# Strassen's seven products for the q, k, v, g projections of layer 0

## The chip, the cores and the metric

The kernel runs on one core of a Trainium2 chip. The metric is the device time of one execution in microseconds, and the comparison is by the median of several runs. All data are float32.

## The reference

The input `x` is 1 x 128 x 256 x 256: 128 rows (`s`) of 256 tokens with 256 channels. Two layers follow each other, each a group norm and an attention over the 256 tokens of each row, added to `x`. Cut to what matters:

```python
# layer 0: 8 heads of 32 channels, with a bias from pair_repr and a gate
gate = sigmoid(xn @ gate_proj)
q, k, v = split(xn @ qkv_proj, 3)            # 256 x 256 each
sim = softmax(q @ k.T / sqrt(32)) + bias     # bias: pair_repr @ bias_proj
x = x + ((sim @ v) * gate) @ out_proj
# layer 1: 4 heads of 64 channels, scores kept only in a band |i - j| <= 16
x = x + softmax(banded(q @ k.T / 8)) @ v @ w_out.T + b_out   # q, k, v with biases
```

The group norm (32 groups of 8 channels) needs statistics over all of `x` before layer 0 starts, and over all of layer 0's output before layer 1 starts.

## The kernel before

There are three stages. The first streams `x` and `pair_repr` through SBUF by DMA: VectorE (DVE) takes the statistics of `x`, TensorE (PE) turns `pair_repr` and forms the bias of the 8 heads, which stays in SBUF (`bias_sb`). The second is layer 0, row by row; its output goes to DRAM (`x1`). The third is layer 1, two rows at a time.

In layer 0 a row lies as channels by tokens: two halves of 128 channels on the partitions, 256 tokens along the free axis. For each row `s`:

- `piece(s, 0)` fetches the row in groups of `XG` = 4 rows (`load`, on SP's queue), turns it on DVE (`turned`, L474) and normalises it on DVE (`normalized`, L464) into `xn`.
- `piece(s, 1..4)` are the projections q, k, v, g. Each is a 256 x 256 by 256 product, made of four matmuls of 128 x 128 weights with 256 columns (`by_channel`, L484; for v `by_token`, L495). ScalarE (ACT) copies each result from PSUM (L542, L547); for g it takes exp(-g) on the way (L552).
- `scores(s, half)` makes the scores of four heads (`sim`, L561), their exponentials on ACT (`ex`, L568) and, on DVE, the sum over the two halves of the keys (`both`, L571).
- `attend(s)` makes the softmax's sums (`zs`, L585), the bias times v (`bv`) and the exponentials times v (`av`, L597). ACT copies `zs` to `z` (L603). DVE forms `d` = (1 + exp(-g)) z (L605), its reciprocal (L609), `t` (L607, L608) and `at` (L611), and a minimum for a check (`zmin`, L613).
- `finish(s)` projects `at` by `out_sb` (`po`, L484), adds the row on DVE (L623), takes the statistics for layer 1 every second row (L626) and stores four rows at a time (L628).

The order of the work is written out in the loop at L635: for each `s` it is scores(s, 0), attend(s - 1), scores(s, 1), the projections of s + 1, finish(s - 1), piece(s + 2, 0). A scheduler may move instructions within this order where the data allow. The PSUM banks are a ring of five that `sim`, the projections and `po` share (`proj_bank`, `sim_bank`), beside one each for `zs`, `bv` and `av`. A bank is taken again when its last reader is done.

GpSimd (POOL) loads the weights and builds masks at the start, and in layer 1 it multiplies the exponentials by the band mask (L717) and adds their halves (L724). It cannot reach PSUM. Weights that need turning are loaded to `w_raw` by `load_weights`, in the first stage.

Of the kernel before, what the change touches and what calls it, by code (L numbers as in the profile page):

```python
# [15 lines left out]
P = 128  # L16
R = 256
# [22 lines left out]
def conv_preact_kernel(  # L40
# [105 lines left out]
    bias_sb = const.tile([P, 2, H0, R], F32, name="bias_sb")  # L146
    zmin = const.tile([P, 2 * S], F32, name="zmin")
# [142 lines left out]
    XG = min(4, S)  # L290
# [7 lines left out]
    GROUPS = [1, 1, 2] + [XG] * (S // XG - 1)  # L298
# [11 lines left out]
    with ExitStack() as early:  # L310
# [6 lines left out]
        w_raw = prt_pool.tile([P, 8, C], F32, name="w_raw", bufs=1)  # L317
# [4 lines left out]
        def load_weights():  # L322
            nc.gpsimd.dma_start(out=w_raw[:, 6:8, :], in_=out_w.rearrange("(t p) c -> p t c", p=P))
# [108 lines left out]
        for m in range(NM):  # L432
# [17 lines left out]
            if m == NM // 4:  # L450
                load_weights()
            if m == NM * 3 // 4:
                turn_weights()
# [48 lines left out]
    SG = min(4, S)  # L502
# [8 lines left out]
    with ExitStack() as both:  # L511
# [5 lines left out]
        def load1(g):  # L517
            if g * XG < S and g not in ygs:
                yg = big1.tile([P, XG, 2, R], F32, tag="yg", name=f"yg{g}", bufs=3)
                nc.sync.dma_start(out=yg, in_=rows(x1, g * XG, XG))  # L520
                ygs[g] = yg

        with ExitStack() as lay0:
# [4 lines left out]
            def piece(s, n):  # L528
                if s >= S:
                    return  # L530
                if n == 0:
                    g, k = ROWS[s]
                    if k == 0:
                        load(g + 1)
                    xt = row.tile([P, 2, R], F32, tag="xt", name=f"xt{s}", bufs=5)
                    turned(xt, xgs[g], k)
                    st[s] = {"xt": xt, "xn": normalized(row, xt, mean0, rstd0, f"0_{s}")}
                elif n in (1, 2):
                    w = "qk"[n - 1]
                    ps = by_channel(qkv_sb, (n - 1) * C, st[s]["xn"], f"p{w}{s}")  # L540
                    a = row.tile([P, 2, R], F32, tag=w, name=f"{w}{s}")
                    nc.scalar.copy(a, ps)  # L542
                    st[s][w] = a
                elif n == 3:
                    ps = by_token(st[s]["xn"], qkv_sb, 2 * C, f"pv{s}")
                    v = row.tile([P, 2, C], F32, tag="v", name=f"v{s}", bufs=3)
                    nc.scalar.copy(v, ps)  # L547
                    st[s]["v"] = v
                elif n == 4:
                    ps = by_channel(gate_sb, 0, st[s]["xn"], f"pg{s}")  # L550
                    e = row.tile([P, 2, R], F32, tag="e", name=f"e{s}", bufs=3)
                    nc.scalar.activation(e, ps, AF.Exp, scale=-1.0)  # L552
                    st[s]["e"] = e

            def scores(s, half):
                q, k = st[s]["q"], st[s]["k"]
                sims = [sim_bank(f"sim{s}_{half}_{j}") for j in range(4)]
                for kt in range(2):
                    for j in range(4):
# [3 lines left out]
                            lhsT=k[p0 : p0 + D0, half, kt * P : (kt + 1) * P], rhs=q[p0 : p0 + D0, half, :],  # L563
# [3 lines left out]
                for j in range(4):  # L567
                    nc.scalar.activation(ex[:, j], sims[j], AF.Exp, scale=1.0 / math.sqrt(D0))  # L568
                both = att.tile([P, 4, R], F32, tag="both", name=f"both{s}_{half}", bufs=3)
                for j in range(0, 4, 2):  # L570
                    nc.vector.tensor_tensor(both[:, j : j + 2], ex[:, j : j + 2, 0, :], ex[:, j : j + 2, 1, :], ALU.add)  # L571
                hd[s, half] = (ex, both)

            def attend(s):
                if s < 0:
                    return
                (ex0, both0), (ex1, both1) = hd.pop((s, 0)), hd.pop((s, 1))
                v = st[s]["v"]

                zs = ps_av.tile([P, 2, R], F32, tag="z", name=f"zs{s}")  # L580
                bv0 = ps_av.tile([P, 2, R], F32, tag="bv", name=f"bv{s}")
                av = ps_av.tile([P, 2, R], F32, tag="av", name=f"av{s}")
                for half, both in enumerate((both0, both1)):
# [5 lines left out]
                for to, weights in (  # L589
# [432 lines left out]
```

## Time and profile before

| | us |
|---|---|
| median of 6 runs | 3367.05 (3364.84 to 3368.4) |
| profiled execution | 3364.23 |
| its span, first to last instruction | 3362.5 |
| PE busy | 3278.7 (98%) |
| DVE busy | 2461.1 (73%) |
| ACT busy | 1479.9 (44%) |
| POOL busy | 416.5 (12%) |

The span is one execution on the core. Matmuls are pipelined and their ends are modelled, so a busy PE is not PE at its peak. A group's line in the profile gives source line, engine, operation, output and inputs, shapes and count, then busy us, mean ns of one, and the idle time before it with what ended it. A float32 matmul shows as two instructions.

### The profile page before, as it was taken

The numbers are of one execution on the slowest core, as the hardware profiler recorded it, in microseconds if no ns is written. First come the engines' busy times: TensorE is split into PE (matmuls) and PEld (weight loads), VectorE is DVE, ScalarE is ACT, GpSimd is POOL, SyncE is SP. The second block draws the span as 40 slices with busy tenths as digits, with TensorE's granted clock in tenths as the row PEclk, the third lists the DMA queues.
The fourth block names the chain that finished last, engine by engine and source line by source line (L and its number), as shares of the span: only waits on it lengthen the run. The fifth ranks groups of instructions, "written<-read, shape, count | busy, mean of one in ns | idle before, by whom it ended". The sixth has DMA issues, their size and how long they took to land.

```text
span 3362.5 us, 83261 instructions
## 1 busy us (share of the span) xinstructions
PE 3278.7 (98%) x36809; PEld 2585.2 (77%) x36809; DVE 2461.1 (73%) x3794; ACT 1479.9 (44%) x3162; POOL 416.5 (12%) x347
## 2 busy tenths in 40 slices
PE   6799999999999999999999999899999999999997
PEld 4477777777777777777777777688888888888886
DVE  4757777777777777777777777657777777777777
ACT  4554444444444444444444444344444444444442
POOL 2000000000000000000000000033333333333332
PEclk9999999999999999999999999999999999999999
DMA  9932212112121121121121110012222122222221
GB/s 382 411 74 51 64 26 51 27 28 49 26 39 39 26 39 39 26 47 30 26 51 27 36 42 14 14 39 54 56 71 58 52 71 58 53 70 58 60 63 40
DMA packets 343296, 209.12 MB, mean 62 GB/s; under 512 B 270600, under 2 KB 336144, under 8 KB 336656
## 3 DMA queue, kind: packets, MB, share of 16 engines
q1 hardware_dynamic: 342032, 201.36, 22.4%
q8 instruction: 290, 4.75, 0.6%
q0 software_dynamic: 752, 2.36, 0.2%
q14 instruction: 78, 0.64, 0.1%
q10 hardware_dynamic: 144, 0.00, 0.0%
HBM read 136.59 MB, written 67.11 MB: 61 GB/s over the span
## 4 chain that ended last, share of the span: by engine, by line
PE 93%; DMA 3%; DVE 3%; issue 0%; ACT 0%; SPq 0%; DVEq 0%; ACTq 0%
PE sim L561 8%; PE pq L484 7%; PE p1v L686 7%; PE 1po L484 7%; PE p1q L484 7%; PE p1k L484 7%; PE po L484 7%; PE pg L484 7%; PE pv L495 7%; PE pk L484 7%; PE bv L597 6%; PE av L597 6%; PE zs L585 4%; DMA xs<-in_x_dram 3%; PE 1sim L707 3%; PE 1avz L739 2%
## 5 line engine op out<-in xcount | busy, mean ns | idle before, releaser
L568 ACT ACTIVATE ex<-sim 128x512 f32<-128x512 f32 x1024 | 528.7, 603 | 643.9 <-PE sim L561 643.6
L764 DVE RECIPROCAL 1rz<-1z 128x512 f32<-128x512 f32 x128 | 427.8, 3342 | 174.1 <-ACT 1z L762 174.1
L609 DVE RECIPROCAL d<-d 128x512 f32<-128x512 f32 x128 | 427.9, 3343 | 0.0
L571 DVE TENSOR_TENSOR both<-ex 128x512 f32<-128x512 f32 x512 | 333.9, 682 | 74.0 <-ACT ex L568 74.0
L717 POOL TENSOR_TENSOR 1p<-1ex,seen 128x768 f32<-128x768 f32 x128 | 233.8, 1827 | 740.4 <-ACT 1ex L715 740.4
L561 PE MATMUL sim<-q,k 32*128 32x256 f32 x4096 | 294.9, 401 | 0.2 <-ACT ex L568 0.2
L464 DVE TENSOR_SCALAR xn<-xt,mean,rstd 128x256 f32<-128x256 f32 x256 | 94.1, 409 | 265.1 <-PE pg L484 265.0
L561 PEld LDWEIGHTS sim<-q,k 32*128 32x128 f32 x4096 | 186.1, 184 | 101.2 <-DVE zmin L613 51.0
L678 ACT ACTIVATE 1q<-p1q,bqk 128x256 f32<-128x256 f32 x256 | 107.2, 470 | 345.3 <-PE p1q L484 345.3
L484 PE MATMUL pq<-xn,qkv_sb 128*128 128x256 f32 x1024 | 255.5, 393 | 0.0
L484 PE MATMUL po<-at,out_sb 128*128 128x256 f32 x1024 | 245.7, 384 | 10.1 <-DVE at L611 10.1
L663 POOL MEMSET 1p<- 128x1216 f32 x4 | 4.3, 1111 | 1997.3 <-DVE at L611 1997.3
L484 PE MATMUL 1po<-1at,w_out_t 128*128 128x256 f32 x1024 | 241.6, 390 | 5.3 <-DVE 1at L766 5.3
L484 PE MATMUL p1q<-xn,w_in_t 128*128 128x256 f32 x1024 | 244.1, 382 | 2.0 <-DVE xn L464 1.1
L597 PE MATMUL bv<-bias_sb,v 128*32 128x256 f32 x4096 | 244.4, 379 | 0.0
L597 PE MATMUL av<-ex,v 128*32 128x256 f32 x4096 | 244.4, 379 | 0.0
L484 PE MATMUL p1k<-xn,w_in_t 128*128 128x256 f32 x1024 | 243.0, 381 | 0.0
L484 PE MATMUL pg<-xn,gate_sb 128*128 128x256 f32 x1024 | 241.9, 379 | 0.0
L495 PE MATMUL pv<-qkv_sb,xn 128*128 128x256 f32 x1024 | 241.9, 379 | 0.0
L484 PE MATMUL pk<-xn,qkv_sb 128*128 128x256 f32 x1024 | 241.9, 379 | 0.0
L686 PEld LDWEIGHTS p1v<-w_in_t,xn 128*64 128x64 f32 x4096 | 222.3, 137 | 21.5 <-issue 21.5
L686 PE MATMUL p1v<-w_in_t,xn 128*64 128x128 f32 x4096 | 238.0, 274 | 0.0
(157 smaller groups left out, 5192.4 us busy)
## 6 DMA issues: line engine op xcount, KB each, us to landing
pr<-in_L_conv_pair_repr_dram SPq DMA_DIRECT2D x32, 1024.0 KB, 23.4
x<-o SPq DMA_DIRECT2D x32, 1024.0 KB, 4.4
yg<-x SPq DMA_DIRECT2D x32, 1024.0 KB, 5.8
out_dram<-1o SPq DMA_DIRECT2D x256, 128.0 KB, 3.6
xg<-in_x_dram SPq DMA_DIRECT2D x124, 256.0 KB, 5.8
xs<-in_x_dram SPq DMA_DIRECT2D x15, 2048.0 KB, 21.4
xs<-in_x_dram SPq DMA_DIRECT2D x2, 1024.0 KB, 17.7
qkv_sb<-in_L_conv_qkv_proj_dram POOLq DMA_DIRECT2D x4, 192.0 KB, 13.1
```

The lines of the kernel that those rows point to most:

```text
L484: nc.tensor.matmul(ps[:, m, :], lhsT=w[:, kt, col + m * P : col + (m + 1) * P], rhs=xn[:, kt, :], start=(kt == 0), stop=(kt == 1),)
L495: nc.tensor.matmul(ps[:, t, :], lhsT=a[:, kt, t * P : (t + 1) * P], rhs=w[:, kt, col : col + C], start=(kt == 0), stop=(kt == 1),)
L561: nc.tensor.matmul(sims[j][:, kt, :], lhsT=k[p0 : p0 + D0, half, kt * P : (kt + 1) * P], rhs=q[p0 : p0 + D0, half, :], start=True, stop=True,)
L568: nc.scalar.activation(ex[:, j], sims[j], AF.Exp, scale=1.0 / math.sqrt(D0))
L571: nc.vector.tensor_tensor(both[:, j : j + 2], ex[:, j : j + 2, 0, :], ex[:, j : j + 2, 1, :], ALU.add)
L585: nc.tensor.matmul(zs[D0 * j : D0 * (j + 1), half, :], lhsT=ones[:, 0:D0], rhs=both[:, j, :], start=True, stop=True,)
L597: nc.tensor.matmul(to[D0 * j : D0 * (j + 1), half, :], lhsT=v[:, kt, h * D0 : (h + 1) * D0], rhs=weights(h, kt), start=(kt == 0), stop=(kt ...
L609: nc.vector.reciprocal(d, d)
L678: nc.scalar.activation(a[:, half, :], ps[:, half, :], AF.Identity, bias=b)
L686: nc.tensor.matmul(ps[KB * half : KB * (half + 1), b, :], lhsT=xn[:, kt, KB * b : KB * (b + 1)], rhs=w_in_t[:, kt, 2 * C + P * half : 2 * ...
L717: nc.gpsimd.tensor_tensor(p.rearrange("p j (r c) -> p (j r) c", c=WROW)[:, :, 0 : 2 * WSTEP] .rearrange("p r (t c) -> p r t c", c=WSTEP)[: ...
L764: nc.vector.reciprocal(rz, z)
```

## The change

Two rows are projected at once. Call the rows A and B, each with its two halves of channels x0 and x1, so that the product with one projection's weights (w00, w10, w01, w11, each 128 x 128) is a 2 x 2 block product. Strassen's scheme with shared sums makes it with seven block products where the plain form has eight. The sums of weights are made once, in the first stage, by GpSimd (`sum_weights`). The four sums of a pair's rows (`sum_rows`, into `ts`) and the last sums of the results (`Seven.add`) are made by GpSimd for each pair.

`stretch` is the new order of two projections, q and k after even rows, v and g after odd ones, for the pair of rows ahead. Each of the two has one PSUM bank in which sums grow over products 1, 5, 6, 3, 7, 4. ACT copies it out (`take`) after 5, after 6, after 7 and after 4, and the products 2 of both go to a third bank, copied as `two`. The exponentials of the second half of the scores (`weigh`) are placed between these steps. exp(-g) is taken in place for a pair of rows at once. A v product has its row sum as the weights, and so is two matmuls with 128 columns.

`attend` is split: `sum_heads` (`zs` and `bv`) stands before scores(s, 1), `av` and the DVE steps after it. The groups of rows are two, not four (`XG`), in `load`, in the stores and in layer 1's loads, where the buffers are five, not three. `w_raw` is taken from the ring of the `pair_repr` tiles. Layer 1's output tile shares the ring of layer 0's.

The diff, cut to its core:

```diff
+    NS = ("s1", "s2", "s3", "s4", "n11")
+    sums = {w: const.tile([P, len(NS), P], F32, name=f"sums_{w}") for w in "qkvg"}
+    def quarter(w, kt, m):
+        source, col = (gate_sb, 0) if w == "g" else (qkv_sb, "qkv".index(w) * C)
+        return source[:, kt, col + m * P : col + (m + 1) * P]
+    def sum_weights():
+        for w in "qkvg":
+            s1, s2, s3, s4, n11 = (sums[w][:, n, :] for n in range(len(NS)))
+            w00, w10, w01, w11 = (quarter(w, kt, m) for m in range(2) for kt in range(2))
+            nc.gpsimd.tensor_tensor(s1, w01, w11, ALU.add)
+            nc.gpsimd.tensor_tensor(s2, s1, w00, ALU.subtract)
+            nc.gpsimd.tensor_tensor(s3, w00, w01, ALU.subtract)
+            nc.gpsimd.tensor_tensor(s4, w10, s2, ALU.subtract)
+            nc.gpsimd.tensor_scalar(n11, w11, -1.0, None, op0=ALU.mult)
+    def stationary(w, n):
+        if n <= 2:
+            return quarter(w, n - 1, 0)
+        return sums[w][:, NS.index({3: "s4", 4: "n11", 5: "s1", 6: "s2", 7: "s3"}[n]), :]
...
-    XG = min(4, S)
+    XG = 2
...
-    GROUPS = [1, 1, 2] + [XG] * (S // XG - 1)
+    GROUPS = [1, 1] + [XG] * (S // XG - 1)
...
-        w_raw = prt_pool.tile([P, 8, C], F32, name="w_raw", bufs=1)
...
         def load_weights():
+            w_raw = pr_pool.tile([P, 8, C], F32, tag="pr", name="w_raw")
...
                 load_weights()
+                sum_weights()
...
-                yg = big1.tile([P, XG, 2, R], F32, tag="yg", name=f"yg{g}", bufs=3)
+                yg = big1.tile([P, XG, 2, R], F32, tag="yg", name=f"yg{g}", bufs=5)
...
+            xns, tss, res = {}, {}, {}
+            def normal(s):
                 if s >= S:
                     return
...
+                g, k = ROWS[s]
+                if k == 0:
+                    load(g + 1)
+                xt = row.tile([P, 2, R], F32, tag="xt", name=f"xt{s}", bufs=6)
+                turned(xt, xgs[g], k)
+                st[s] = {"xt": xt}
+                i, r = divmod(s, 2)
+                if r == 0:
+                    xns[i] = row.tile([P, 4, R], F32, tag="xn", name=f"xn{i}")
+                for half in range(2):
+                    nc.vector.tensor_scalar(
+                        xns[i][:, 2 * r + half, :], xt[:, half, :],
+                        mean0[:, half : half + 1], rstd0[:, half : half + 1],
+                        op0=ALU.subtract, op1=ALU.mult,
+                    )
+            def sum_rows(i):
+                if 2 * i >= S:
+                    return
+                x, t = xns[i], row.tile([P, 4, R], F32, tag="ts", name=f"ts{i}", bufs=1)
+                nc.gpsimd.tensor_tensor(t[:, 0], x[:, 2], x[:, 0], ALU.subtract)
+                nc.gpsimd.tensor_tensor(t[:, 1], x[:, 3], t[:, 0], ALU.subtract)
+                nc.gpsimd.tensor_tensor(t[:, 2], x[:, 3], x[:, 2], ALU.subtract)
+                nc.gpsimd.tensor_tensor(t[:, 3], t[:, 1], x[:, 1], ALU.subtract)
+                tss[i] = t
+            class Seven:
+                def __init__(self, w, i):
+                    self.w, self.i = w, i
+                    self.to = row.tile([P, 4, R], F32, tag=w, name=f"{w}{i}")
+                    res[w, i] = self.to
+                    self.mid = row.tile([P, 2, R], F32, tag="mid", name=f"mid{w}{i}")
+                def open(self):
+                    self.ps = proj_bank(f"p{self.w}{self.i}")
+                def product(self, n, two=None):
+                    x, t = xns[self.i], tss[self.i]
+                    moving = {1: x[:, 0], 2: x[:, 1], 3: x[:, 3], 4: t[:, 3], 5: t[:, 0], 6: t[:, 1], 7: t[:, 2]}[n]
+                    out = two if n == 2 else self.ps[:, 1 if n in (3, 5) else 0, :]
+                    first = n == 1 or (n == 2 and self.w in "qv")
+                    flags = dict(stop=n in (2, 3, 4), skip_group_check=True)
+                    if self.w != "v":
+                        nc.tensor.matmul(out, lhsT=stationary(self.w, n), rhs=moving, start=first, **flags)
+                        return
+                    for t2 in range(2):
+                        cols = slice(t2 * P, (t2 + 1) * P)
+                        nc.tensor.matmul(
+                            out[:, cols], lhsT=moving[:, cols], rhs=stationary(self.w, n),
+                            start=first and t2 == 0, **flags
+                        )
+                def take(self, what):
+                    if what == "15":
+                        nc.scalar.copy(self.to[:, 0:4:3, :], self.ps)
+                    elif what == "6":
+                        nc.scalar.copy(self.mid[:, 0, :], self.ps[:, 0, :])
+                    elif what == "7":
+                        nc.scalar.copy(self.mid[:, 1, :], self.ps[:, 0, :])
+                    else:
+                        nc.scalar.copy(self.to[:, 1:3, :], self.ps)
+                def add(self, two):
+                    nc.gpsimd.tensor_tensor(self.to[:, 0], self.to[:, 0], two, ALU.add)
+                    nc.gpsimd.tensor_tensor(self.to[:, 2:4], self.to[:, 2:4], self.mid, ALU.add)
...
+                def weigh(j):
                     nc.scalar.activation(ex[:, j], sims[j], AF.Exp, scale=1.0 / math.sqrt(D0))
-                both = att.tile([P, 4, R], F32, tag="both", name=f"both{s}_{half}", bufs=3)
-                for j in range(0, 4, 2):
-                    nc.vector.tensor_tensor(both[:, j : j + 2], ex[:, j : j + 2, 0, :], ex[:, j : j + 2, 1, :], ALU.add)
+                    if j % 2 == 1:
+                        nc.vector.tensor_tensor(
+                            both[:, j - 1 : j + 1], ex[:, j - 1 : j + 1, 0, :], ex[:, j - 1 : j + 1, 1, :], ALU.add
+                        )
+                return weigh
...
+            def products(to, s, weights):
+                i, r = divmod(s, 2)
+                v = res["v", i]
+                for half in range(2):
+                    for kt in range(2):
+                        for j in range(4):
+                            c0 = kt * P + j * D0
+                            nc.tensor.matmul(
+                                to[D0 * j : D0 * (j + 1), half, :],
+                                lhsT=v[:, 2 * r + half, c0 : c0 + D0], rhs=weights(4 * half + j, kt),
+                                start=(kt == 0), stop=(kt == 1),
+                            )
+            def sum_heads(s):
                 if s < 0:
                     return
                 zs = ps_av.tile([P, 2, R], F32, tag="z", name=f"zs{s}")
                 bv0 = ps_av.tile([P, 2, R], F32, tag="bv", name=f"bv{s}")
+                for half in range(2):
+                    both = hd[s, half][1]
                     for j in range(4):
                         nc.tensor.matmul(
                             zs[D0 * j : D0 * (j + 1), half, :], lhsT=ones[:, 0:D0], rhs=both[:, j, :],
                             start=True, stop=True,
                         )
+                products(bv0, s, lambda h, kt: bias_sb[:, kt, h, :])
+                hd[s] = (zs, bv0)
...
+            def stretch(names, i, weigh=None, s=-1):
+                weigh = weigh or (lambda j: None)
+                if 2 * i >= S:
+                    for j in range(4):
+                        weigh(j)
+                    if s >= 0:
+                        finish(s, by_channel(out_sb, 0, st[s]["at"], f"po{s}"))
+                    return
+                f, g = (Seven(w, i) for w in names)
+                f.open()
+                f.product(1)
+                f.product(5)
+                weigh(0)
+                g.open()
+                g.product(1)
+                g.product(5)
+                weigh(1)
+                f.take("15")
+                twos = proj_bank(f"p2{names}{i}")
+                f.product(2, twos[:, 0, :])
+                g.product(2, twos[:, 1, :])
+                g.take("15")
+                weigh(2)
+                f.product(6)
+                g.product(6)
+                f.take("6")
+                weigh(3)
+                f.product(3)
+                g.product(3)
+                g.take("6")
+                two = row.tile([P, 2, R], F32, tag="two", name=f"two{names}{i}")
+                nc.scalar.copy(two, twos)
+                f.product(7)
+                g.product(7)
+                f.take("7")
+                g.take("7")
+                f.product(4)
+                g.product(4)
+                f.take("34")
+                g.take("34")
+                po = by_channel(out_sb, 0, st[s]["at"], f"po{s}") if s >= 0 else None
+                for n, p in enumerate((f, g)):
+                    p.add(two[:, n, :])
+                if s >= 0:
+                    finish(s, po)
+            for s in range(2):
+                normal(s)
+            sum_rows(0)
+            stretch("qk", 0)
+            for s in range(2, 4):
+                normal(s)
             for s in range(S + 1):
                 if s < S:
-                    scores(s, 0)
+                    weigh = scores(s, 0)
+                    if s == 0:
+                        stretch("vg", 0, weigh)
+                        sum_rows(1)
+                    else:
+                        for j in range(4):
+                            weigh(j)
+                sum_heads(s - 1)
+                weigh = scores(s, 1) if s < S else None
                 attend(s - 1)
-                if s < S:
-                    scores(s, 1)
-                for n in range(1, 5):
-                    piece(s + 1, n)
-                finish(s - 1)
+                if s % 2 == 0 and s < S:
+                    e = res["g", s // 2]
+                    tc.keep_in_program_order(nc.scalar.activation(e, e, AF.Exp, scale=-1.0))
+                stretch(("qk", "vg")[s % 2], s // 2 + 1, weigh, s - 1)
                 if s == S - 2:
                     most1 = join_most(st1, stats1, 1)
                     load1(0)
                     load1(1)
-                piece(s + 2, 0)
+                if s % 2 == 1:
+                    normal(s + 3)
+                    normal(s + 4)
+                    sum_rows((s + 3) // 2)
...
-                    o = big1.tile([P, 2, 2, R], F32, tag="o1", name=f"1o{s}")
+                    o = big1.tile([P, 2, 2, R], F32, tag="o", name=f"1o{s}")
```

In the built program PE's order in a row is: sim (half 0), zs, bv, sim (half 1), av, products 1 and 5 of the first matrix, 1 and 5 of the second, both 2, both 6, 3 of the second, 3 of the first, both 7, the first matmul of `po`, both 4, the rest of `po`. DVE's order is: `o`, in every second row the statistics, the transposes and `xn` of a row ahead, both `both` of half 0, `d`, `zmin`, the reciprocal, the two `t`, the first `both` of half 1, `at`, the second `both`.

## The prediction

> **What bounds the kernel now.** First the engines' busy time and the chain that ended last: TensorE is busy nearly all the span, and the chain runs through it.
>
> ```profile
> PE 3278.7 (98%) x36809; PEld 2585.2 (77%) x36809; DVE 2461.1 (73%) x3794; ACT 1479.9 (44%) x3162; POOL 416.5 (12%) x347
> PE 93%; DMA 3%; DVE 3%; issue 0%; ACT 0%; SPq 0%; DVEq 0%; ACTq 0%
> ```
>
> Then the windows by stage (length, then busy us and instructions of each engine, granted clock, DMA share and GB/s). The stage of layer 0's rows, which the change rewrites, has PE busy in 1955.8 of 1956 us at full clock. DVE is the runner-up, and GpSimd does nothing in it.
>
> ```profile
> 202.00:2158.00 1956.00, 1955.76 (x19220) 1455.43 (x19219) 1472.41 (x2022) 882.43 (x1777) 0.00 (x0) 1.00 0.17 36
> ```
>
> Last the timeline of one row of that stage (start, length, engine, line, operation): from one first `sim` to the next.
>
> ```profile
> 1200.65 1.15 PE L561 MATMUL sim<-q,k 32*128 32x256 f32 x16
> 1201.73 1.07 PE L585 MATMUL zs<-both,ones 128*32 128x256 f32 x16
> 1202.61 1.91 PE L597 MATMUL bv<-bias_sb,v 128*32 128x256 f32 x32
> 1204.34 1.91 PE L597 MATMUL av<-ex,v 128*32 128x256 f32 x32
> 1206.18 1.15 PE L561 MATMUL sim<-q,k 32*128 32x256 f32 x16
> 1207.26 2.00 PE L484 MATMUL pq<-xn,qkv_sb 128*128 128x256 f32 x8
> 1209.09 1.89 PE L484 MATMUL pk<-xn,qkv_sb 128*128 128x256 f32 x8
> 1210.81 1.89 PE L495 MATMUL pv<-qkv_sb,xn 128*128 128x256 f32 x8
> 1212.54 1.89 PE L484 MATMUL pg<-xn,gate_sb 128*128 128x256 f32 x8
> 1214.27 1.89 PE L484 MATMUL po<-at,out_sb 128*128 128x256 f32 x8
> 1216.09 1.15 PE L561 MATMUL sim<-q,k 32*128 32x256 f32 x16
> ```
>
> And the lines of DVE's timeline in the same row that count below:
>
> ```profile
> 1201.48 1.29 DVE L626 BATCH_NORM_STATS2 stats<-o 128x6 f32<-128x512 f32 x2
> ...
> 1205.73 3.34 DVE L609 RECIPROCAL d<-d 128x512 f32<-128x512 f32 x1
> ...
> 1210.45 0.69 DVE L611 TENSOR_TENSOR at<-t,d 128x512 f32<-128x512 f32 x1
> ...
> 1214.47 0.73 DVE L464 TENSOR_SCALAR xn<-xt,mean,rstd 128x256 f32<-128x256 f32 x2 [2.12 <-PE pg L484]
> ```
>
> A row takes 15.44 us, and PE goes from group to group without a hole. `at`, which `po` needs, is done at 10.5 us into the row (1211.14), and `po` starts at 13.6. So DVE has 3.1 us in hand. That margin is what the change spends.
>
> **The sum goes against the profiled execution**: 3364.2 us, its span 3362.5 and 1.7 around it. That is 2.8 below the median of 3367.05, added back at the end. A measurement of this kernel can tell about 0.2% from no change, 6.7 us.
>
> **Removed.** The four projections are 32 instructions per row, 0.216 us apart (pk to pv: 1.72 for 8). Seven products for eight leave 28: 0.863 us off a row, 110.5 over 128 rows. A row bound by PE is then 14.58. The built program has these 28, so the change does what it says.
>
> **v in halves.** Each v product is two matmuls of 128 columns, so a full weight load comes every half step: 28 loads in a pair of rows where 14 wider steps would do. Two rows bound this, p1v of layer 1 on the page (busy us, mean ns) and pz in the timeline of the first stage:
>
> ```profile
> L686 PE MATMUL p1v<-w_in_t,xn 128*64 128x128 f32 x4096 | 238.0, 274 | 0.0
> ```
>
> ```profile
> 171.66 3.66 PE L389 MATMUL pz<-ident,pr 128*128 128x128 f32 x32
> ```
>
> pz has full 128x128 loads at 128 columns: (3.66 - 0.3)/31 = 0.108 a step, just half of 0.216, so no loss. p1v (two halves side by side) is 238/2048 = 0.116, or 0.22 us a pair, 14 in all. I take pz: 0. The 14 stays in the range.
>
> **ScalarE and the accumulators.** One bank is evacuated four times in the middle of its sums (after products 5, 6, 7 and 4), so PE and ScalarE take turns on it. ScalarE's copies per row go from four of 0.6 to five of 0.6 and four of 0.47, and every second row gets an exponential of 128x1024 (about 1.1): some 10 us in a row with the rest, not a bound. The turn counts. In the built order q's product 3 waits until its product 6 is copied out: ScalarE starts 0.2 after the next group has begun on PE (pk at 1209.09, the copy of q at 1209.29), its copy takes 0.47 (L678's mean) and may first have to wait for the copy of both products 2, and only k's 6 and 3 (0.86) lie between. Likewise 4 after 7, where the first step of `po` was placed as filler. I count 0.1 a row, bounds 0 and 0.4 (each turn short by 0.2): 12.6 us, 126 rows.
>
> **DVE's margin.** Counted from the row's first `sim`, three things move `at`. `xn` now stands ahead of the two `both` of half 0, 0.65 later. One `both` of half 1 stands ahead of `at`, 0.6 later. `av` moves behind the second `sim`, which DVE, still in its reciprocal, does not feel. So in rows with the statistics (1.2 us, every second) `at` ends at 10.5 + 1.25 = 11.75, in the others near 11.0. And `po` is wanted sooner: av ends near 6.6, then twelve products of 0.432, so its first step falls at 11.8, and products 4 of both matrices are queued behind it. The 3.1 us are gone: 0 to 0.1 left.
>
> **GpSimd.** Per pair of rows it gets four row sums and, for each matrix, an add of 256 and one of 512 elements. Its nearest rows:
>
> ```profile
> L717 POOL TENSOR_TENSOR 1p<-1ex,seen 128x768 f32<-128x768 f32 x128 | 233.8, 1827 | 740.4 <-ACT 1ex L715 740.4
> L724 POOL TENSOR_TENSOR 1zp<-1p 128x512 f32<-128x512 f32 x128 | 162.6, 1270 | 10.0
> ```
>
> The step is 2.18 ns an element beside 0.15 fixed, so 0.71 us for 256. 8 x 0.71 + 4 x 1.27 = 10.8 us in 29: the work fits, and q, k, v, g have a row's slack. The row sums come ready by about 5 us of a row, products 5 wait for them at 7.0. So nothing is lost by GpSimd's own time.
>
> What it may cost is on DVE. The first two adds of a stretch start when the copy of both products 2 is out, at 10.1 us, and run to 11.5. That is just when DVE does `both` and `at`, each reading two SBUF tensors, as GpSimd does. No row shows the two together: GpSimd was idle in layer 0, and layer 1's DVE steps read at most one tensor of SBUF. Those are no slower for it (xn 411 ns in layer 1, 409 in layer 0), so the lower end is 0. The upper end is that each step shuts the other out for its whole length, in turns. Odd rows: `both` (due 10.4) waits to 10.8, `at` waits for the second add, 12.0 to 12.7, and `po` is 0.9 late: 15.49 a row. Even rows come to the same, since GpSimd's late adds and row sums already push `both` of half 0. In between, only the part that grows with size excludes (0.56 of 0.71 for GpSimd, 0.53 of 0.60 for DVE): `both` to 10.65, second add from 11.2, `at` from 11.75 to 12.4, `po` 0.54 late: 15.12 a row. I take this one. The layer 1 rows argue for 0 but are of another kind, and two engines on the same memory for the same half microsecond argue for a price. Below nothing it cannot be: a wait shortens no step.
>
> The Trainium skill speaks against the change here. Its page "SBUF — State Buffer", section "Who interferes with whom", says that a VectorE instruction with two SBUF inputs and a GpSimd instruction that reads SBUF shut each other out, the first keeping the shared pair for the whole instruction. No row of this trace shows it or denies it. By that rule the sum would be the upper end, 3380, by layer 1's rows 3278.
>
> **Ends.** Start: two rows must be normalised and a GpSimd sum made before product 5, and row 0 carries two stretches: 3 us. End: row 126 has no projections left to cover it. PE has 8.5 us of work there, while `at` and `po` need about 13.5: 5 us. The weights' staging tile takes one of the five `pr` buffers while DMA is the bound (396 GB/s): 0 to 2.6 us (1 MB at that rate), 1 taken. Twenty weight sums run on an idle GpSimd early: 0. Groups of two rows, not four, double the issues on SP and halve each load. A group is still fetched one pair (29 us) ahead and xg landed in 5.8 us: 0. Together 9.
>
> **Sum:** 3364.2 - 110.5 + 126 x 0.54 + 9 = 3330.7, and 2.8 for the median: **3334**. (The 0.1 of ScalarE's turns falls within the later wait for `at`.)
>
> **Rivals.**
> *No contention.* The 0.54 is then 0.1: 3364.2 - 110.5 + 12.6 + 9 + 2.8 = 3278. For it: layer 1's unchanged DVE steps. Against: they read one tensor.
> *Full exclusion (slower).* One mechanism, at the wait of `po` for `at`: 0.91 a row, 3380. Where DVE also loses each tie it is 1.26 (15.84 a row), 3424. It decides against the change from 0.81 us a row on, (110.5 - 9)/126. For it: DVE's margin is gone and all falls at the one spot. Against: it needs whole instructions, start-up included, to exclude.
>
> **How the numbers follow.** Partial exclusion 0.38, no contention 0.26, full exclusion 0.28, something unpriced and worse 0.08. The range takes the first two and full exclusion with some of its ties: 3265 to 3400. Faster by over 0.2% (below 3360): 0.26 and most of 0.38, 0.58. Within 0.2%: the edges of both, 0.08. Slower: 0.34.
>
> **What would show it.** A row near 15.1 us, 14.6 to 14.7 without contention, 15.5 with all of it. PE idle ahead of `po` released by DVE `at`, once a row. `at` ending past 12 us of its row, `both` or `at` longer than 0.69, or GpSimd's adds longer than 0.71 and 1.27 where they overlap. Product 3 released by ScalarE with some 0.1. v products at 0.108 a step; 0.116 or more would cost up to 14. I am wrong in the mechanism if PE waits most for ScalarE or GpSimd and not for `at`, or if the row is below 14.5.

## The result, and the profile after

The changed kernel takes 3373.59 us (median of 16 runs, 3369.86 to 3376.66) against 3365.65 for the kernel before (36 runs): a ratio of 1.0022, 95% interval 1.0016 to 1.0029. It is a little slower, at the edge of what can be told from no change, and 40 us above the forecast of 3334. The profiled execution took 3372.7 us, its span 3371.0.

The page's busy line and its chain of work that ended last:

```profile
PE 3232.6 (96%) x37193; PEld 2493.2 (74%) x37193; DVE 2640.8 (78%) x3794; ACT 1781.1 (53%) x3866; POOL 1210.4 (36%) x1135
PE 69%; DVE 26%; DMA 3%; issue 1%; ACT 0%; POOL 0%; SPq 0%; DVEq 0%; POOLq 0%; ACTq 0%
```

PE has less to do (3232.6 us, 3278.7 before), as intended. But the chain, which had 3% of DVE before, now has 26%. DVE runs the same number of instructions as before and is busy 180 us longer. The window over layer 0's rows shows both: PE is no longer full (1899 of 1956 us), and GpSimd, idle before, works 779 us.

```profile
204.00:2160.00 1956.00, 1898.89 (x19595) 1359.21 (x19594) 1649.41 (x2019) 1180.82 (x2476) 779.42 (x761) 1.00 0.14 36
```

A row no longer has one period. From one first `sim` to the next, rows in which q and k are projected take 15.70 to 15.77 us, 15.74 on the mean (these are the rows without the statistics on DVE, "even rows" in the prediction), and rows with v and g take 15.06. Before, every row took 15.44. The timeline of a q, k row on PE, from `sim` to `sim`:

```profile
1225.79 1.15 PE L640 MATMUL sim<-q,k 32*128 32x256 f32 x16
1226.86 1.07 PE L681 MATMUL zs<-both,ones 128*32 128x256 f32 x16
1227.75 1.91 PE L667 MATMUL bv<-bias_sb,v 128*32 128x256 f32 x32
1229.59 1.15 PE L640 MATMUL sim<-q,k 32*128 32x256 f32 x16
1230.67 1.93 PE L667 MATMUL av<-ex,v 128*32 128x256 f32 x32
1232.53 0.70 PE L610 MATMUL pq<-xn,qkv_sb 128*128 128x256 f32 x2
...
1237.38 0.59 PE L610 MATMUL pk<-ts,sums_k 128*128 128x256 f32 x2
1238.80 0.67 PE L513 MATMUL po<-at,out_sb 128*128 128x256 f32 x2 [0.82 <-DVE at L705]
```

Products step from 1232.53 on without a hole, then `po` starts 1.42 after the last one where 0.43 is the pitch of two steps: PE waits about 1 us for `at`. A second thing is easy to miss: bv to `sim` is now 1.84 and not 1.73.

DVE in the same row, and the last lines of the v, g row ahead of it:

```profile
1221.05 0.68 DVE L653 TENSOR_TENSOR both<-ex 128x512 f32<-128x512 f32 x1
1221.65 1.22 DVE L705 TENSOR_TENSOR at<-t,d 128x512 f32<-128x512 f32 x1
1222.79 1.21 DVE L653 TENSOR_TENSOR both<-ex 128x512 f32<-128x512 f32 x1
...
1227.32 1.47 DVE L573 TENSOR_SCALAR xn<-xt,mean,rstd 128x256 f32<-128x256 f32 x2
1228.71 2.36 DVE L653 TENSOR_TENSOR both<-ex 128x512 f32<-128x512 f32 x2
1230.99 0.68 DVE L699 SCALAR_TENSOR_TENSOR d<-g,z 128x512 f32<-128x512 f32 x1
...
1236.78 1.26 DVE L653 TENSOR_TENSOR both<-ex 128x512 f32<-128x512 f32 x1
1237.97 0.68 DVE L705 TENSOR_TENSOR at<-t,d 128x512 f32<-128x512 f32 x1
```

And GpSimd at the same time:

```profile
1221.07 1.25 POOL L630 TENSOR_TENSOR v<-v,twovg 128x256 f32<-128x256 f32 x1 [8.80 <-ACT twovg L756]
1222.28 1.17 POOL L630 TENSOR_TENSOR g<-g,twovg 128x256 f32<-128x256 f32 x1
...
1226.61 1.29 POOL L631 TENSOR_TENSOR g<-g,midg 128x512 f32<-128x512 f32 x1
1227.85 0.79 POOL L585 TENSOR_TENSOR ts<-xn,ts 128x256 f32<-128x256 f32 x1
1228.60 0.78 POOL L586 TENSOR_TENSOR ts<-xn 128x256 f32<-128x256 f32 x1
1229.34 1.18 POOL L587 TENSOR_TENSOR ts<-ts,xn 128x256 f32<-128x256 f32 x1
1236.09 0.73 POOL L630 TENSOR_TENSOR q<-q,twoqk 128x256 f32<-128x256 f32 x1 [5.57 <-ACT twoqk L756]
1236.77 0.73 POOL L630 TENSOR_TENSOR k<-k,twoqk 128x256 f32<-128x256 f32 x1
```

Read the two together. `both` starts at 1221.05, the addition to v at 1221.07. `both` takes its usual 0.68 and ends at 1221.73; the addition takes 1.25 and ends 0.59 after it. `at`, issued at 1221.65, in turn stands until the addition's end, 1222.32, takes 1.22 and ends 0.55 after it. At 1227.3 to 1231 four operations of DVE stand behind GpSimd's last addition and the row sums one after the other: `xn` takes 1.47 (0.69 in the row with the statistics), two `both` 2.36 (1.29 there). `d` then starts 5.20 us into the row; without GpSimd's work (below) it starts at 3.87. At 1236.78 the addition to k has the start, and `both`, ahead of `at`, loses 0.6 more.

### The profile page after: what moved, and what is told of

Its sections match the earlier page's. It is cut to its first block, busy times and chain, and to the rows that moved or that the text cites. A ratio compares the mean times of both kernels' runs of the same rounds, so it can differ in the third digit from the quotient of the medians.

```text
span 3371.0 us, 86569 instructions
## 1 busy us (share of the span) xinstructions
PE 3232.6 (96%) x37193; PEld 2493.2 (74%) x37193; DVE 2640.8 (78%) x3794; ACT 1781.1 (53%) x3866; POOL 1210.4 (36%) x1135
## 3 DMA queue, kind: packets, MB, share of 16 engines
q0 software_dynamic: 752, 2.36, 0.2%
## 4 chain that ended last, share of the span: by engine, by line
PE 69%; DVE 26%; DMA 3%; issue 1%; ACT 0%; POOL 0%; SPq 0%; DVEq 0%; POOLq 0%; ACTq 0%
PE po L513 7%; PE p1v L838 7%; PE 1po L513 7%; PE p1q L513 7%; PE p1k L513 7%; DVE d L703 6%; DVE both L653 6%; PE pv L614 5%; PE pg L610 5%; PE sim L640 4%; PE av L667 3%; PE bv L667 3%; PE 1sim L859 3%; DVE xn L573 3%; PE 1avz L891 2%; DMA xs<-in_x_dram 2%
## 5 line engine op out<-in xcount | busy, mean ns | idle before, releaser
L653 DVE TENSOR_TENSOR both<-ex 128x512 f32<-128x512 f32 x512 | 458.5, 915 | 24.5 <-ACT ex L651 24.5
L513 PE MATMUL po<-at,out_sb 128*128 128x256 f32 x1024 | 276.0, 393 | 56.8 <-DVE at L705 56.2
L714 DVE TENSOR_TENSOR o<-po,xt 128x512 f32<-128x512 f32 x128 | 88.6, 692 | 283.0 <-PE po L513 283.0
L513 PEld LDWEIGHTS po<-at,out_sb 128*128 128x128 f32 x1024 | 186.8, 192 | 124.9 <-PE pk L610 72.1
L630 POOL TENSOR_TENSOR v<-v,twovg 128x256 f32<-128x256 f32 x64 | 77.6, 1212 | 556.9 <-ACT twovg L756 556.9
L513 PEld LDWEIGHTS 1po<-1at,w_out_t 128*128 128x128 f32 x1024 | 192.1, 193 | 55.2 <-ACT 1z L914 23.5
L513 PEld LDWEIGHTS p1q<-xn,w_in_t 128*128 128x128 f32 x1024 | 195.3, 191 | 29.5 <-issue 1.3
L513 PEld LDWEIGHTS p1k<-xn,w_in_t 128*128 128x128 f32 x1024 | 195.2, 191 | 26.8
```

The lines of the kernel that those rows point to most:

```text
L513: nc.tensor.matmul(ps[:, m, :], lhsT=w[:, kt, col + m * P : col + (m + 1) * P], rhs=xn[:, kt, :], start=(kt == 0), stop=(kt == 1),)
L653: nc.vector.tensor_tensor(both[:, j - 1 : j + 1], ex[:, j - 1 : j + 1, 0, :], ex[:, j - 1 : j + 1, 1, :], ALU.add)
```

## The experiments

The theory: GpSimd's operations that read SBUF and VectorE's operations that read two SBUF tensors exclude each other, and the time lost ends at `po`. The rival: the seven products themselves cost more than counted. The table gives the measured row periods (from the starts of PE's `sim` groups in the traces; of the changed kernel's q, k rows the mean, otherwise the median) and times; the kernel before took 3364.6 to 3364.7 beside them. Runs with one time were taken once.

| kernel | q, k row | v, g row | time |
|---|---|---|---|
| before | 15.44 | 15.44 | 3365.65 |
| after | 15.74 | 15.06 | 3373.59 |
| no GpSimd work | 14.71 | 14.82 | 3287.66 |
| no additions | 14.71 | 14.82 | 3289.04 |
| no row sums | 14.71 | 15.06 | 3308.89 |
| fills in place of the work | 14.71 | 14.82 | 3289.35 |
| only row sums moved | 14.71 | 15.06 | 3308.06 |
| only additions moved | 15.30 | 14.82 | 3330.23 |
| both moved | 14.71 | 14.82 | 3296.40 (4 runs) |
| both moved, av first | 14.73 | 14.77 | 3294.55 |
| the same, copies first | 14.57 | 14.68 | 3280.31 (4 runs) |

**Without GpSimd's work, all of it and by halves.** The edits to the changed kernel:

```diff
 def sum_rows(i):
+    if i > 0:
+        tss[i] = tss[0]
+        return
...
 def add(self, two):
+    return
```

The values of these three kernels, and of the one with fills below, are not the right ones. So in all four the branch at the end of the program that would make the work anew (`tc.If(sure < P)`) is shut with `sure < 0`.

> The changed kernel without GpSimd's work in layer 0's rows: the sums of rows are made for the first pair alone and used again for every pair, and the additions to the seven products' results are left out (the matmuls, ScalarE's copies and VectorE's work stay as they are). Theory 1, GpSimd's two-input operations and VectorE's operations on SBUF exclude each other and the lost time ends at `po`: `both` is back at 680 to 690 ns, `xn` at 410, the rows with and without statistics come to the same period of 14.6 to 14.7 us, and the time is 126 x 0.75 = 95 us below the changed kernel's 3371, about 3276. Rival, the seven products themselves cost more than counted (turns of the banks through ScalarE, the 16 copies a pair, the weight loads of 128 x 128): the alternation of 15.06 and 15.74 stays, and the time is within 10 us of 3371.

> GpSimd makes the sums of rows but the additions to the products' results are left out. Theory 1: what is left is 2.9 us of GpSimd for a pair of rows, which meets `xn` of the next pair and the first `both` of the row that has statistics; `xn` stays near 0.58, and the rows come to 14.6 and 14.9 to 15.1 us, 3285 to 3305 in all. Rival (the products): within 10 us of 3371.

> GpSimd makes the additions to the products' results but the sums of rows are made for the first pair alone. Theory 1: the additions of v and g at the end of the row with statistics still meet `xn` and the first `both`, those of q and k meet the first `both` of the row after; the row without statistics is the longer still, 15.1 to 15.4 us, the other near 14.9, and the time is 3310 to 3345. The two losses of this kernel and of the one without additions add up to some 95 us if the two parts act apart. Rival (the products): within 10 us of 3371.

Measured: 3287.66, 3289.04 and 3308.89. The alternation is gone with GpSimd's work, and PE waits for `at` no more. In the kernel without it, DVE's groups in the stage of the rows (busy us, mean ns) read

```profile
L655 DVE TENSOR_TENSOR both<-ex 128x512 f32<-128x512 f32 x492 | 333.0, 688 | 23.0 <-ACT ex L653 19.4
L573 DVE TENSOR_SCALAR xn<-xt,mean,rstd 128x256 f32<-128x256 f32 x242 | 84.5, 393 | 0.0
```

where the changed kernel has, in its own,

```profile
L653 DVE TENSOR_TENSOR both<-ex 128x512 f32<-128x512 f32 x490 | 441.8, 922 | 1.5 <-ACT ex L651 1.5
L573 DVE TENSOR_SCALAR xn<-xt,mean,rstd 128x256 f32<-128x256 f32 x244 | 132.3, 583 | 0.3
```

So nearly all of the wait is GpSimd's doing. Four expectations were off. The row came to 14.76 on average, not to 14.6 or 14.7, and the time 12 us higher than forecast: something on PE itself was missing (below). Without row sums it is the v, g row that stays long, by 0.25, not the other. Without additions `xn` takes 0.41 on the mean, not near 0.58. And the parts don't add up: the additions alone cost 21 us over the kernel without any, the row sums alone 1, both together 86 (the 83 in an expectation below counts from the changed kernel's span).

**Fills in place of the work.** Each addition becomes two fills of the tile that it would have read, and each row sum two fills of its result:

```diff
-nc.gpsimd.tensor_tensor(self.to[:, 0], self.to[:, 0], two, ALU.add)
-nc.gpsimd.tensor_tensor(self.to[:, 2:4], self.to[:, 2:4], self.mid, ALU.add)
+nc.gpsimd.memset(two, 0.0)
+nc.gpsimd.memset(two, 0.0)
+nc.gpsimd.memset(self.mid, 0.0)
+nc.gpsimd.memset(self.mid, 0.0)
...
+nc.gpsimd.memset(t[:, n], 0.0)
+nc.gpsimd.memset(t[:, n], 0.0)
```

> In place of GpSimd's additions and of its sums of rows (after the first pair) stand fills of constants on tiles of the same places, two for each, in the same queue and behind the same copies: about as much busy time of GpSimd (0.33 us for 256 elements, 0.55 for 512, twice each, 9.6 us a pair where the additions and sums are 10.8), but nothing is read. The products therefore get zeros for row sums, and the additions are left out. If it is GpSimd's reading that excludes VectorE, `both` stays at 680 to 690 ns, PE does not wait for `at`, and the time is that of the kernel without the work, 3287 to 3291. If any work of GpSimd on SBUF does, `both` lengthens to 0.85 to 0.95 and the time is 3340 to 3375.

Measured: 3289.35, all rows as without the work. Two of DVE's groups and two of the fills:

```profile
L662 DVE TENSOR_TENSOR both<-ex 128x512 f32<-128x512 f32 x502 | 339.3, 686 | 24.5 <-ACT ex L660 21.1
L573 DVE TENSOR_SCALAR xn<-xt,mean,rstd 128x256 f32<-128x256 f32 x242 | 84.2, 391 | 0.0
```

```profile
L587 POOL MEMSET ts<- 128x256 f32 x244 | 68.9, 312 | 0.0
L639 POOL MEMSET midq<- 128x512 f32 x62 | 32.5, 524 | 54.2 <-ACT midq L632 54.2
```

Neither engine stretches the other, though they meet: of the rows from 400 to 2000 us, `at` ran beside a fill in every one and took 0.685 on the mean, and 164 of the `both` did at 0.683. So for `both` and `at` it isn't GpSimd's work as such, nor its writing: it is its reading. (No fill ran beside `xn`, so this run says nothing on `xn`.) This is what the Trainium skill says, on the page "SBUF — State Buffer", section "Who interferes with whom": an operation of GpSimd that only writes doesn't contend with a VectorE operation with two SBUF inputs, one that reads does, and whoever issues first keeps the shared ports for its whole instruction. The timelines above agree that the second waits for the end of the first; of its own 0.69 or 0.72 it then needs only 0.55 or 0.59 more.

**GpSimd's work moved in time.** Nothing is left out. A copy of one column that reads `d` (or `at`) stands in GpSimd's queue ahead of the row sums (or of the additions), so these can't start before it. `d` is done when DVE goes into `zmin`, the reciprocal (3.34) and the two `t`, which read one SBUF tensor each.

```diff
+def after(what, n):
+    tc.keep_in_program_order(nc.gpsimd.tensor_copy(gate[:, n : n + 1], what[:, 0, 0:1]))
...
 nc.vector.scalar_tensor_tensor(d, e, 1.0, z, op0=ALU.add, op1=ALU.mult)
+if pair is not None:
+    after(d, 0)
+    sum_rows(pair)
...
 po = by_channel(out_sb, 0, st[s]["at"], f"po{s}") if s >= 0 else None
+if s >= 0:
+    after(st[s]["at"], 1)
 for n, p in enumerate((f, g)):
     p.add(two[:, n, :])
...
-sum_rows((s + 3) // 2)
```

> The whole computation, with GpSimd's work moved in time: a copy of one column that reads `d` stands ahead of the sums of rows, so that they run beside the `t` and the reciprocal of the row that uses them, and one that reads `at` stands ahead of the additions. Theory 1: `xn` of the row without statistics no longer meets the sums of rows, but still meets additions; the long row falls from 15.74 to 15.0 to 15.3, the short one stays at 15.0 to 15.1, and the time is 3310 to 3345. If only the quantity of GpSimd's work counts and not its place (it loses as much time wherever it runs), the time stays within 10 us of 3371. If the sums come too late for the products that read them, PE waits at L610 for GpSimd, and it is slower than 3371.

> The kernel with both parts of GpSimd's work moved, timed in rounds beside the kernel before: 3293 to 3298, a ratio of 0.979 to 0.980.

> The whole computation; of GpSimd's work only the sums of rows are moved (behind a copy of one column that reads `d`), the additions stay where the change put them. Without the row sums the additions cost 21 us, without the additions the row sums cost 1, and both together 83. If the rest, 61, comes from the row sums being pushed by the additions of v and g onto `xn` and the first `both` of the next row, this kernel falls to near the 3309 of the kernel without row sums, 3305 to 3320. If it comes from the mere amount of GpSimd's work, or from the additions alone being later with more work ahead of them, it stays above 3345.

> The whole computation; only the additions are moved (behind a copy of one column that reads `at`), the sums of rows stay where the change put them. The additions then start after `at`, so `both` of half 1 and `at` are undisturbed and the row with statistics falls from 15.06 to 14.71 to 14.8. The additions of v and g run 3.9 us from there, the row sums after them, up to some 7 us into the next row, past `xn`, the first `both` and `d`. Theory: GpSimd's work costs only what it takes from VectorE ahead of `at`; `xn` and the first `both` of the row without statistics still lose 0.7 to 1.4 us, and that row is 15.0 to 15.5: 3310 to 3340. If the row sums in this place cost nothing (their product waits for nothing, and the row is 14.8), it is 3288 to 3300; then the loss of 0.25 in the other row, at `both` and `at`, was what pushed them.

Measured: 3295.45 and again 3296.40 (3295.7 to 3297.75, ratio 0.9798, interval 0.9781 to 0.9814) with both moved; 3308.06 with the row sums alone moved; 3330.23 with the additions alone. Both moved is better than expected: its rows are those of the kernel without the work, though the quantity of GpSimd's work is the same. Of the 86 us, place accounts for 77; the other 9 fall outside the rows (from the second row to the last it is 1861.1 us with and without the work). The row sums now run beside the reciprocal, and neither is longer for it:

```profile
1220.09 0.18 POOL L691 COPY gate<-d 128x1 f32<-128x1 f32 x1 [2.39 <-DVE d L704]
1220.23 0.73 POOL L584 TENSOR_TENSOR ts<-xn 128x256 f32<-128x256 f32 x1
1222.42 0.73 POOL L587 TENSOR_TENSOR ts<-ts,xn 128x256 f32<-128x256 f32 x1
```

```profile
1220.54 3.35 DVE L711 RECIPROCAL d<-d 128x512 f32<-128x512 f32 x1
```

`xn` still meets an addition (0.51 on the mean, 0.39 without the work), but at a place where it costs nothing: VectorE would otherwise have waited for `ex` there (21 us of such waits over the rows without the work, 4 here).

The two halves show how the places interact. With the row sums alone moved, the q, k row is at its floor, and what stays is the 0.25 in the v, g row: the addition to v against `both` and `at`, as in the kernel without row sums. With the additions alone moved that 0.25 goes, but the additions to v and g, now later, push the row sums further into the q, k row, and it keeps 0.59. There the timeline shows a victim that was free in the changed kernel, `d`:

```profile
1238.72 1.60 DVE L573 TENSOR_SCALAR xn<-xt,mean,rstd 128x256 f32<-128x256 f32 x2
1240.24 1.82 DVE L653 TENSOR_TENSOR both<-ex 128x512 f32<-128x512 f32 x2
1241.98 1.22 DVE L704 SCALAR_TENSOR_TENSOR d<-g,z 128x512 f32<-128x512 f32 x1
```

**The missing piece on PE.** Without GpSimd's work a row was still 0.18 longer than 14.58. In the steps of its trace one instruction with 256 columns of the products, or four of sim, zs, bv or av together, take 0.216. But where the shape of the stationary operand changes (32x128 for sim, 128x32 for zs, bv and av, 128x128 for the products) the step ahead of the change takes 0.1 more, and the one behind it 0.02 (zs, av) to 0.1 (sim, the products). From zs to bv and, in the kernel before, from bv to av the operands change and the shape doesn't, and the step is the usual one. A row of before has four such changes: po to sim, sim to zs, av to sim, sim to pq. The change put the second `sim` between bv and av, which followed each other in one shape, and there are five: po to sim, sim to zs, bv to sim, sim to av, av to pq. The kernel before with that alone:

```diff
 for to, weights in ((bv0, ...), (av, ...)):
+    if to is av:
+        weigh()          # scores(s, 1)
...
-attend(s - 1)
-if s < S:
-    scores(s, 1)
+attend(s - 1, (lambda: scores(s, 1)) if s < S else (lambda: None))
```

> The kernel before, with one thing of the change in it alone: the second `sim` of a row stands between bv and av. Theory: one more change of shape on PE in a row, 0.11 to 0.14 us on 15.44, 15.55 to 15.58, and 14 to 18 us on the whole, 3379 to 3383. Rival: what is missing in the row of the changed kernel lies in the products themselves, and this kernel's time is that of the kernel before within 3 us.

Measured: 3380.13, 15.5 us above the 3364.64 beside it, a row of 15.57. The cost of the move is shown, in a kernel without any other part of the change; that it lies in the shape is read from the steps. Its timeline has the same 1.84 from bv to `sim`:

```profile
1212.77 1.91 PE L600 MATMUL bv<-bias_sb,v 128*32 128x256 f32 x32
1214.61 1.15 PE L561 MATMUL sim<-q,k 32*128 32x256 f32 x16
```

**Undoing it in the better version.** In the kernel with GpSimd's work moved, two lines change places:

```diff
 sum_heads(s - 1)
-weigh = scores(s, 1) if s < S else None
 attend(s - 1, s // 2 + 1 if s % 2 == 0 and s > 0 else None)
+weigh = scores(s, 1) if s < S else None
```

> The kernel with both parts of GpSimd's work moved, and in addition `av` again ahead of the second `sim` of the row, as in the kernel before. In the kernel with GpSimd's work moved PE never waits, yet a row is 14.76 us and not 14.58: the step between matmuls is 0.31 and not 0.196 where the shape of the stationary operand changes (bv to sim, sim to av), and the change makes one such change more in a row. Theory: 0.11 to 0.14 less a row, 14.62 to 14.65, 3278 to 3281 in all. Rival: ScalarE gets the second `sim` 1.9 us later and is late with the copies between the products; PE then waits for ScalarE at L610 or for VectorE at `po`, and the time is 3295 or more.

Measured: 3294.55, a miss; the rival held, to half a us. bv and av take 7.13 us a pair of rows, not 7.41, but product 6 now waits. PE first, then ScalarE:

```profile
1015.63 1.03 PE L610 MATMUL p2qk<-xn,qkv_sb 128*128 128x256 f32 x4
1016.57 0.67 PE L610 MATMUL pq<-ts,sums_q 128*128 128x256 f32 x2
1017.08 0.59 PE L610 MATMUL pk<-ts,sums_k 128*128 128x256 f32 x2
```

```profile
1013.88 2.06 ACT L651 ACTIVATE ex<-sim 128x512 f32<-128x512 f32 x4 [1.95 <-PE sim L640]
1015.81 0.62 ACT L621 COPY q<-pq 128x512 f32<-128x512 f32 x1
```

Four steps of 0.216 from 1015.63 would end at 1016.49; product 6 starts at 1016.57 and its group spreads over 0.51, not 0.43. ScalarE's copy of products 1 and 5, which it needs, ends at 1016.43, since four exponentials stand ahead of it. So the last exponential goes behind the first two copies, and ScalarE's operations of a stretch are kept in the order written:

```diff
+weigh(2)
 f.take("15")
...
 g.take("15")
-weigh(2)
+weigh(3)
...
 f.take("6")
-weigh(3)
```

> The kernel with both parts of GpSimd's work moved and `av` ahead of the second `sim`, with one more edit: ScalarE makes the last exponential of half 1 after the first two copies of products and not ahead of them. In the kernel without this edit PE's groups bv and av take 0.14 less a row, as expected, but product 6 steps 0.29 and 0.295 behind the products 2 (0.216 otherwise), since ScalarE's four exponentials end 0.15 too late for its copy of products 1 and 5. Theory: that copy comes 0.5 earlier, the hole closes, and a row is 14.62 to 14.66 us: 3278 to 3283. Rival: the exponential then delays the copies after product 6 and the hole moves to product 3, or the later `both` delays zs: 3290 to 3297, as without the edit.

Measured: 3280.31 us (3277.04 to 3281.77), a ratio of 0.9751 to the kernel before, interval 0.9735 to 0.9767. This version beats both kernels. Its chain has DVE back at 3%, and the timeline of a row steps without a hole from product to product into `po`:

```profile
PE 92%; DMA 3%; DVE 3%; ACT 0%; issue 0%; POOL 0%; SPq 0%; DVEq 0%; POOLq 0%
```

```profile
1008.84 1.03 PE L610 MATMUL p2qk<-xn,qkv_sb 128*128 128x256 f32 x4
1009.70 0.59 PE L610 MATMUL pq<-ts,sums_q 128*128 128x256 f32 x2
...
1011.86 0.59 PE L610 MATMUL pk<-ts,sums_k 128*128 128x256 f32 x2
1012.29 0.59 PE L513 MATMUL po<-at,out_sb 128*128 128x256 f32 x2
```

## Why the prediction was wrong

The mechanism that it weighed most, a late `at` through GpSimd's reading, was there, and so was the gain on PE. It failed in three terms that all point the same way. Counted per pair of rows, from the starts of PE's matmuls (mean of some 50 pairs; the kernel without GpSimd's work gives the part that is PE's alone):

| term, us per pair | predicted | measured |
|---|---|---|
| projections and `po` on PE | -1.73 | -1.59 |
| bv and av on PE | 0 | +0.28 |
| wait for `at` | +1.08 | +1.28 |
| sum | -0.65 | -0.03 |

The difference, 0.62 a pair, is 39 us over 63 pairs, out of the 42 between the sum's 3330.7 and the profiled 3372.7.

- **bv and av (17 us of the miss)** is the largest, and it was overlooked, not mis-sized. The text says that av moves behind the second `sim`, but follows this on DVE alone; on PE the move counted as nothing. The row of before shows the price to whoever asks: av to `sim` is 1.84, bv to av 1.73. It also sinks "a row bound by PE is then 14.58": without GpSimd's work it is 14.71 with q and k, 14.82 with v and g. With av first again and the copies ahead it is 14.57 and 14.68.
- **The wait (13 us)** was taken as 0.54 in every row, and that failed in both rows, in opposite directions: 0.25 with v and g, 1.03 with q and k. The sum of a pair came near (1.28 for 1.08) by luck, since the two errors offset each other. The price of one meeting was not the error. "Only the part that grows with size excludes" put 0.53 of VectorE's 0.60 and 0.56 of GpSimd's 0.71 behind the other's; in the changed kernel `at` ends 0.55 after the GpSimd operation that it met (73 cases, 0.545 to 0.554), and a GpSimd operation of 256 columns 0.59 after the `both` or `at` that it met (158 cases, 0.58 to 0.59). What failed is which operations meet. In the v, g row `both` won the start over the addition to v by 0.02 us, so one addition stood ahead of `at` and not two: `at` ends 12.14 us into the row, for 12.4 predicted. "Even rows come to the same" is the step with the larger error: there `at` ends at 12.86. `xn` was not priced at all, and the row sums, which alone cost 1 us in 3289, are held up by the additions to v and g and meet `xn` and both `both` of half 0, so that `d` starts 1.33 late. At the end of that row `both`, in some rows `at`, loses once more, to the addition to k. That PE waits no longer for so late an `at` is because it wants it later: without GpSimd's work `po` starts at 12.0 and 12.1, not at 11.8.
- **Projections (9 us).** v in halves was taken at 0.108 a step from pz. It measures 0.1115 inside a group, and without GpSimd's work a v, g row is 0.105 longer than a q, k row: 7 us in all, between the two bounds given. The rest is one row: at 1134.9 us of the kernel without GpSimd's work VectorE joins half of the statistics (two operations of 0.99), `at` is late, and the row takes 16.35. Before, VectorE's margin covered this, and every row took 15.44.
- **ScalarE's turns** were taken at 0.1 a row, absorbed by the later wait. They cost nothing: without GpSimd's work PE steps at 0.216 through products 6, 3, 7 and 4. They do bind as soon as the exponentials come later (the run with av first).
- **Right:** GpSimd's durations (0.72 and 1.27 for 0.71 and 1.27), the place of the wait, `xg`'s loads and the weight sums at nothing, and the ends. Layer 1's first product starts 7.0 us later than before (2199.9, 2192.9) and the rows gave 1.7, so start and end of the rows cost 8.7; 9 was predicted.
- **The rivals.** "No contention" (3278) is 10 us below the kernel without GpSimd's work (3287.66): the overlooked 17 us and v's 7 are missing in it, and 12.6 for ScalarE's turns are too much. What spoke for it, layer 1's `xn` at 411 ns, said nothing: none of those 256 operations runs beside GpSimd in the trace of before. "Full exclusion" (3380) is near to the measured time, but by luck: it takes 0.91 in every row, 1.82 a pair where 1.28 was measured, and the 17 us are missing in it too. The argument for the middle value, that a start-up share might not exclude, rested on no row; the 0.55 and 0.59 bear out its sizes.

## What to carry to other kernels

When work moves to GpSimd, lay it out against VectorE's timeline: every reading operation of it that meets a two-input VectorE operation delays one of the two (here by 0.53 to 0.58 us when they start together, for operations of 0.69 and 0.72), and what counts is how much falls ahead of the step that the bound engine waits for. The place matters more than the amount: here the same work cost 86 us where it fell by itself and 9 behind one-column copies that hold it until VectorE's reciprocal or past `at`. And when an edit reorders TensorE's groups, price each change in the shape of the stationary operand, even where the number of steps is the same.

## What the runs showed of the hardware

- `xn`, a `tensor_scalar` with one SBUF tensor and two columns as operands, is excluded too: 0.39 alone, 0.78 on the mean (104 cases, up to 1.02) behind GpSimd's additions and row sums. The prediction left it out. (The section of the Trainium skill named above lists `tensor_scalar` among the operations that can take the shared ports; the trace agrees in the time, and does not show the mode. It does show that `xn` ends 0.15 after the GpSimd operation, with 256 columns, where `at` ends 0.55 after it with 512, so a column costs `xn` little more than half as much there.) The reciprocal (3.34), the transposes, the statistics, and the `t` and `o` that read PSUM kept their times.
- Two operations that start within 0.02 us of each other run in turn: 0.68 for the first, 1.25 for the second, which ends 0.59 after the first.
- A copy of one column on GpSimd took 0.18 behind `d`, but 0.51 to 0.58 behind `at`, where a `both` was running: it stood until `both` was over.
